# Seven block products for eight in a two-layer graph network's adjacency products, with the order of all engines computed by list scheduling

## The chip, the cores and the metric

The kernel runs on one core of one Trainium2 chip. A core has five engines that matter here, each with a queue of its own that it works through in order: PE (TensorE: matmuls and weight loads), DVE (VectorE), ACT (ScalarE), POOL (GpSimd) and SP, which only issues transfers (DMA). They meet through semaphores. The metric is the device time of one execution in microseconds (us), as a median over runs.

## The reference

There are 64 graphs of 256 nodes with 512 features each. For every graph two layers are computed, both on a normalised and rectified copy of x, and each is added to x:

```python
# layer 0
h = maximum(layernorm(x), 0)
agg = einsum('bij,bjf->bif', adj, h) / maximum(sum(adj), 1e-6)
x = x + relu(concat([h, agg], 2) @ W.T)
# layer 1
h = maximum(layernorm(x), 0)
Xw = h @ Wv + bv
e = leaky_relu((Xw @ aw[:d])[:, None, :] + (Xw @ aw[d:])[:, :, None] + ab, 0.2)
al = adj * exp(e)
transition = al / (sum(al) + 1e-12)
H = 0
for k in range(3):
    H = H + h @ Wk[k] + bk[k]
    h = einsum('bij,bjd->bid', transition, h)
x = x + relu(H)
```

All of it is in fp32. The three products that the change is about multiply a 256 x 256 matrix (the scaled adjacency once, the transition twice) by a 256 x 512 matrix.

## The kernel before, in words

Everything is split by 128 partitions: the 256 nodes into NC = 2 blocks, the 512 features into FC = 4. The nodes are split by parity, so that the last index of a transposed tile such as `h0t` or `ant` says which node block a column belongs to.

A graph goes through these pieces, each a generator whose `yield`s cut it into steps:

- `prepare(g)`: norm of x (`norm_relu`: statistics at L187 on DVE, variance on POOL at L192 and L194, the factor nmr at L197 on DVE, the scaled and rectified copy at L200 on ACT), transposition by 32 x 32 blocks on DVE (L215) and through DRAM (L220 out, L225 back) into `h0t`, and the same for the scaled adjacency (`scaled`, L290 to L296) into `ant`. `blocks` (L233 to L236, POOL) makes four sums of blocks of `h0t`.
- `layer0(g)`: `seven` multiplies h with the two halves of the weight in seven block products of 512 columns (14 matmuls) and leaves one half in `q`, the other in two banks of PSUM; `spread` adds the adjacency times `q` to those banks in four matmuls; L332 adds x and the rectified sum into a new buffer `x1`.
- `turn1(g)`: norm, transposition and block sums of x1, into `h1t`.
- `own(g)`: `seven` with the third-width weights (258 columns: 256 of Wk[0] and one column each for the attention vectors), into `e`; L356 to L359 make `sj` and `si`.
- `transition(g)`: `sj` goes to DRAM and comes back in every partition (`row`); ACT makes two exponentials (L377); DVE takes their maximum (L380), multiplies by the adjacency and sums (L384); ACT scales (L393); the result is transposed through DRAM into `tt`.
- `pair(g)`: `seven` for Wk[2] and Wk[1], into `q1` and two banks.
- `twice(g)`: transition times `q1` onto those banks (`spread`), copies into `u` (L425, ACT), then transition times `u` onto banks that DVE has filled with `e` plus the biases (`seed`, L415), and L433 adds x1 and the rectified sum into `o`, which is stored.

`seven` computes a product of 2 x 2 blocks with seven block multiplications instead of eight. Weights were summed once at the start (`combine`, L93); blocks of h are summed per graph. Partial results stay in three PSUM banks p, r and d, and ACT copies them from one to another between the matmuls (L252, L255, L257, L265). All matmuls of `seven` and `spread` are issued through one helper, so they all carry line 240.

The order on every engine is written out by hand: the strings FIRST, TURN and LAST (L487 to L498) name the pieces by letter and take one step of each in turn; TURN is repeated for the graphs 4 to 63, with up to four graphs in flight. `tc.manual_schedule` keeps that order on all five engines. The setup of the weights stands in `weights_l0` and `weights_l1`; there L159 multiplies two SBUF tiles on DVE, next to POOL's `combine`.

Of the kernel before, what the change touches and what calls it, by code (L numbers as in the profile page):

```python
# [23 lines left out]
def bcast(ap, offset, n):  # L24

    return bass.AP(tensor=ap.tensor, offset=ap.offset + offset, ap=[[0, P], [1, n]])
# [3 lines left out]
def gnn_two_layers(ctx: ExitStack, tc: tile.TileContext, x, adj, w0, wv, bv, aw, ab, wk, bk, out):  # L30

# [7 lines left out]
    const = ctx.enter_context(tc.tile_pool(name="const", bufs=1))  # L56
    loads = ctx.enter_context(tc.tile_pool(name="loads", bufs=3))
    early = ctx.enter_context(tc.tile_pool(name="early", bufs=2))
    small = ctx.enter_context(tc.tile_pool(name="small", bufs=4))
    work = ctx.enter_context(tc.tile_pool(name="work", bufs=1))  # L60
    psum = ctx.enter_context(tc.tile_pool(name="psum", bufs=1, space=bass.MemoryType.PSUM))
    banks0 = [psum.tile([P, F], FP, name=f"bank0_{i}") for i in range(3)]
    banks1 = [psum.tile([P, F], FP, name=f"bank1_{i}") for i in range(3)]
    banks2 = [psum.tile([P, F], FP, name=f"bank2_{i}") for i in range(2)]
    dram = ctx.enter_context(tc.tile_pool(name="dram", bufs=2, space=bass.MemoryType.DRAM))

    X, A = {}, {}

    def load(g, what):
        if what is X:  # L70
            X[g] = loads.tile([P, NC, F], FP, name="x")
            nc.sync.dma_start(X[g], x[g].rearrange("(c p) f -> p c f", p=P))
        else:
            A[g] = loads.tile([P, NC, N], FP, name="a", bufs=4)
            nc.sync.dma_start(A[g], adj[g].rearrange("(c p) j -> p c j", p=P))
# [3 lines left out]
    def forms(name, width):  # L79

        return {k: const.tile([P, FC // 2, width], FP, name=f"{name}_{k}") for k in names}

    B0, B1, B2 = forms("l0", F), forms("l1", F), forms("l1s", HW)
    bk_sb = const.tile([P, F], FP, name="bk_sb")
    c0 = const.tile([P, 1], FP, name="c0")
    ident = const.tile([P, P], FP, name="ident")
    mhalf = const.tile([P, NC], FP, name="mhalf")
    zero = const.tile([P, F], BF, name="zero")

    def combine(b, b12, eng=(nc.vector,) * 4):  # L90

        for e, to, x, y in zip(eng, ("t3", "t1", "t2", "t4"), ("b22", None, "b22", "b21"), (None, "b11", "t1", "t2")):
            e.tensor_sub(b[to], b12 if x is None else b[x], b12 if y is None else b[y])  # L93
            yield

    def turned_on_pe(blocks, banks):

        for i in range(0, len(blocks), FC):
            pt = next(banks).rearrange("p (k n) -> p k n", k=FC)
            for k, block in enumerate(blocks[i : i + FC]):  # L100
                nc.tensor.transpose(pt[:, k, :], block, ident)  # L101
            yield pt

    def weights_l0(w0_sb, b12, banks):

        for side, to in enumerate(((B0["b11"], B0["b21"]), (b12, B0["b22"]))):
            pts = turned_on_pe([w0_sb[oc][:, (side * FC + k) * P :][:, :P] for oc in range(FC) for k in range(FC)], banks)
            for oc, pt in enumerate(pts):
                for kh in range(2):
                    (nc.scalar.copy if oc % 2 else nc.vector.tensor_copy)(to[kh][:, :, oc * P : (oc + 1) * P],  # L110
                                                                         pt[:, 2 * kh : 2 * kh + 2, :])

    def flipped_on_pe(src, width, banks, pool, name, bufs=1):

        t = pool.tile([P, width // P, P, NC], FP, name=name, bufs=bufs)
        for c in range(NC):
            for pt in turned_on_pe([src[:, c, k * P : (k + 1) * P] for k in range(width // P)], banks):
                (nc.scalar.copy if c else nc.vector.tensor_copy)(t[:, :, :, c], pt[:, : width // P, :])
        return t

    def spare(name, bufs=1):

        return work.tile([P, 2, F], FP, name=name, bufs=bufs).rearrange("p s f -> p (s f)")

    def weights_l1():


        aw_sb = spare("x1", 4).rearrange("p (s f) -> p s f", s=2)
        wv_sb = [work.tile([P, NC, 2, HW], FP, name="e", bufs=2).rearrange("p c s w -> p (c s w)")[:, : 2 * F]
                 .rearrange("p (c f) -> p c f", c=2) for _ in range(2)]  # L130
        b12s = spare("u")[:, : FC // 2 * HW].rearrange("p (c w) -> p c w", w=HW)
        b12 = spare("o").rearrange("p (c f) -> p c f", f=F)
        scr, bv_sb = (work.tile([P, F], FP, name=n) for n in ("z0", "z1"))
        two = work.tile([P, FC, P, NC], FP, name="h1t", bufs=2).rearrange("p k n c -> p (k n c)")
        biases = [two[:, :F], two[:, F:], work.tile([P, F], FP, name="tt")]
        vc = small.tile([P, 2, FC], FP, name="vc", bufs=1)
        cc = small.tile([P, 2], FP, name="cc", bufs=1)
        ab_sb = small.tile([P, 1], FP, name="ab_sb", bufs=1)
        src = [wk[k].rearrange("(h c p) o -> h p c o", p=P, h=2) for k in range(NW)]
        nc.sync.dma_start(aw_sb, bcast(aw, 0, 2 * F))  # L140
        for h in range(2):
            nc.sync.dma_start(wv_sb[h], wv.rearrange("(h c p) o -> h p c o", p=P, h=2)[h])
        halves = ((b12s, 0, 1), (B2["b22"], 1, 1), (B2["b11"], 0, 0), (B2["b21"], 1, 0))
        for to, kh, col in halves:
            nc.sync.dma_start(to[:, :, :half], src[0][kh][:, :, col * half : (col + 1) * half])
            nc.gpsimd.memset(to[:, :, half + 1], 0.0)
        yield
        for to, k, kh in ((b12, 2, 0), (B1["b22"], 2, 1), (B1["b11"], 1, 0), (B1["b21"], 1, 1)):
            nc.sync.dma_start(to, src[k][kh])
        nc.sync.dma_start(bv_sb, bcast(bv, 0, F))  # L150
        nc.sync.dma_start(ab_sb, bcast(ab, 0, 1))
        for k in range(NW):
            nc.sync.dma_start(biases[k], bcast(bk, k * F, F))
        yield
        sums = combine(B1, b12, (nc.gpsimd,) * 4)
        for c in range(FC):
            next(sums)
            for s in range(2):
                nc.vector.scalar_tensor_tensor(scr, wv_sb[c // 2][:, c % 2, :], 1.0, aw_sb[:, s, :], op0=ALU.mult,  # L159
                                               op1=ALU.mult, accum_out=vc[:, s, c : c + 1])  # L160
            yield
        for to, kh, col in halves:
            nc.vector.tensor_copy(to[:, :, half], vc[:, col, 2 * kh : 2 * kh + 2])
        yield from combine(B2, b12s)
        for s in range(2):
            nc.vector.scalar_tensor_tensor(scr, bv_sb, 1.0, aw_sb[:, s, :], op0=ALU.mult, op1=ALU.mult,
                                           accum_out=cc[:, s : s + 1])
        nc.vector.scalar_tensor_tensor(c0, cc[:, 0:1], cc[:, 1:2], ab_sb, op0=ALU.add, op1=ALU.add)
        nc.vector.tensor_add(bk_sb, biases[0], biases[1])
        nc.vector.tensor_add(bk_sb, bk_sb, biases[2])  # L170
        yield


    def finished(steps):

        while True:
            try:
                next(steps)
            except StopIteration as end:
                return end.value  # L180

    def norm_relu(src):

        stats = small.tile([P, NC, 6], FP, name="stats")
        mv = small.tile([P, NC, 2], FP, name="mv")
        for c in range(NC):
            nc.vector.bn_stats(stats[:, c, :], src[:, c, :])  # L187
            nc.vector.bn_aggr(mv[:, c, :], stats[:, c, :])  # L188
            if c == 0:
                yield  # L190
        ve = small.tile([P, NC], FP, name="ve")
        nc.gpsimd.tensor_scalar(ve, mv[:, :, 1], LN_EPS, None, op0=ALU.add)  # L192
        rstd = small.tile([P, NC], FP, name="rstd")
        nc.gpsimd.tensor_tensor(rstd, ve, mhalf, op=ALU.pow)  # L194
        yield
        nmr = small.tile([P, NC], FP, name="nmr")
        nc.vector.scalar_tensor_tensor(nmr, mv[:, :, 0], -1.0, rstd, op0=ALU.mult, op1=ALU.mult)  # L197
        h = early.tile([P, NC, F], FP, name="h", bufs=1)
        for c in range(NC):
            nc.scalar.activation(h[:, c, :], src[:, c, :], AF.Relu, bias=nmr[:, c : c + 1],  # L200
                                 scale=rstd[:, c : c + 1])
            yield
        return h

    class Flip:


# [239 lines left out]
    def first(tr_banks):  # L447
# [16 lines left out]
        for _ in range(3):  # L464
            next(sums)
# [82 lines left out]
```

## Time and profile before

| what | value |
|---|---|
| median of 3 runs | 2643.75 us (2642.53 to 2643.8) |
| profiled execution: span | 2643.6 us; the page gives no other time of it |
| PE busy | 2612.3 us, 99% |
| DVE busy | 1204.4 us, 46% |
| ACT busy | 897.2 us, 34% |
| POOL busy | 524.2 us, 20% |
| PE weight loads (PEld) | 1347.6 us, 51%, beside PE's matmuls |
| DMA | 46.3% of 16 engines' time, 112 GB/s to and from memory |
| granted TensorE clock, mean | 0.997 |

Busy time is the union of an engine's instructions in the trace. Matmuls are pipelined: a 512-column fp32 matmul appears as two records, each some 0.59 us long, while the next one starts 0.43 us after it. So the length of a record says little and the distance between starts says much. In a group's row the numbers are: how often, busy us, mean ns of one, and the idle time of the engine just before it with what ended that. For PE the idle time ahead of matmuls is 25 us in all, all but 0.3 of it in the first 150 us.

### The profile page before, as it was taken

To read this page: it belongs to the slowest core of one execution; us is meant where nothing else is said; L and a number is where in the kernel's file an instruction comes from. 1 tells how busy PE (TensorE), PEld (TensorE's weight loads), DVE (VectorE), ACT (ScalarE), POOL (GpSimd) and SP (SyncE) were. 2 spreads that over 40 slices of the span, in tenths; PEclk is the share of its full clock that TensorE was granted. 3 is DMA by queue.
4 is the path that set the end of the run, shared out by engine and by line. 5 is a ranking of instruction groups with operands and counts; after the bars stand their busy time and mean duration, and the time that the engine had idled before them with its cause. 6 is when DMAs were issued, how large, how long until landed. Compare 5 with 4: busy or idle time off the path is not lost.

```text
span 2643.6 us, 23486 instructions
## 1 busy us (share of the span) xinstructions
PE 2612.3 (99%) x6983; PEld 1347.6 (51%) x6983; DVE 1204.4 (46%) x2664; ACT 897.2 (34%) x1807; POOL 524.2 (20%) x785
## 2 busy tenths in 40 slices
PE   7999999999999999999999999999999999999999
PEld 3544555555545545555555455555555554555554
DVE  5544444444444444444444444444444444444433
ACT  2333333333333333333333333333333333333332
POOL 3311211221121112111211221121112112211210
PEclk9999999999999999999999999999999999999999
DMA  5444454454454444444444445444445454454421
GB/s 183 108 126 119 108 118 110 111 123 106 120 120 100 121 115 112 116 111 112 123 103 123 116 103 122 113 112 116 111 114 123 100 125 116 104 122 109 110 74 44
DMA packets 576222, 298.93 MB, mean 113 GB/s; under 512 B 418784, under 2 KB 540640, under 8 KB 576096
## 3 DMA queue, kind: packets, MB, share of 16 engines
q1 hardware_dynamic: 576096, 297.44, 46.3%
q8 instruction: 56, 0.92, 0.1%
q14 instruction: 70, 0.57, 0.1%
HBM read 165.15 MB, written 132.19 MB: 112 GB/s over the span
## 4 chain that ended last, share of the span: by engine, by line
PE 97%; DVE 1%; issue 0%; ACT 0%; DMA 0%; SPq 0%; POOL 0%; DVEq 0%; ACTq 0%
PE bank L240 97%; PE bank L101 0%; DVE z L159 0%; DVE l_t L93 0%; DMA x<-in_x_dram 0%; DMA row<-ds 0%; DVE turned L215 0%; SPq L220 0%; DVE stats L187 0%; ACT z L377 0%; DVE nmr L197 0%; DVE o L433 0%; ACT an L296 0%; DVE l1s_t L93 0%; POOL rstd L194 0%
## 5 line engine op out<-in xcount | busy, mean ns | idle before, releaser
L240 PE MATMUL bank<-l_t,h1t_s 128*128 128x512 f32 x780 | 367.4, 594 | 0.7 <-ACT bank L252 0.7
L240 PE MATMUL bank<-l_t,h0t_s 128*128 128x512 f32 x756 | 356.9, 595 | 4.1 <-DVE l_t L93 3.4
L252 ACT COPY bank<-bank 128x512 f32<-128x512 f32 (+1 forms) x192 | 95.9, 499 | 710.7 <-PE bank L240 710.7
L215 DVE STREAM_TRANSPOSE turned<-h 128x512 f32<-128x512 f32 x252 | 178.4, 709 | 298.0 <-ACT h L200 298.0
L233 POOL TENSOR_TENSOR h0t_s<-h0t 128x256 f32<-128x256 f32 x63 | 53.3, 847 | 982.9 <-DMA h0t<-dh0t 880.3
L240 PE MATMUL bank<-l_b,h1t 128*128 128x512 f32 x520 | 244.4, 592 | 0.1
L240 PE MATMUL bank<-u,tt 128*128 128x512 f32 x512 | 242.1, 596 | 2.3 <-ACT u L425 2.3
L240 PE MATMUL bank<-q,tt 128*128 128x512 f32 x512 | 240.0, 592 | 1.3 <-DMA tt<-dtt 1.3
L240 PE MATMUL bank<-q,ant 128*128 128x512 f32 x512 | 232.5, 596 | 5.3 <-DVE q L275 5.3
L240 PEld LDWEIGHTS bank<-l_t,h0t_s 128*128 128x128 f32 x756 | 143.8, 191 | 183.5 <-issue 169.1
L240 PE MATMUL bank<-l_b,h0t 128*128 128x512 f32 x504 | 237.2, 593 | 0.0
L192 POOL TENSOR_SCALAR ve<-mv 128x2 f32<-128x2 f32 x128 | 29.2, 228 | 1020.4 <-DVE mv L188 1011.8
L200 ACT ACTIVATE h<-x,nmr,rstd 128x512 f32<-128x512 f32 x256 | 202.2, 818 | 17.7 <-DVE nmr L197 17.7
L240 PEld LDWEIGHTS bank<-l_t,h1t_s 128*128 128x128 f32 x780 | 147.7, 190 | 109.7 <-issue 97.0
L240 PEld LDWEIGHTS bank<-l1s_t,h1t_s 128*128 128x128 f32 x768 | 146.5, 191 | 102.7 <-issue 84.1
L240 PE MATMUL bank<-l1s_t,h1t_s 128*128 128x258 f32 x768 | 198.7, 381 | 0.0
L268 DVE TENSOR_TENSOR q<-bank,m 128x512 f32<-128x512 f32 x128 | 88.5, 692 | 202.2 <-PE bank L240 201.2
L332 DVE SCALAR_TENSOR_TENSOR x<-bank,x 128x512 f32<-128x512 f32 x128 | 88.5, 692 | 197.7 <-PE bank L240 197.7
L187 DVE BATCH_NORM_STATS2 stats<-x 128x6 f32<-128x512 f32 x256 | 172.2, 673 | 5.0 <-DMA x<-in_x_dram 5.0
L240 PEld LDWEIGHTS bank<-q,ant 128*128 128x128 f32 x512 | 100.8, 197 | 124.3 <-issue 109.4
L240 PEld LDWEIGHTS bank<-u,tt 128*128 128x128 f32 x512 | 100.6, 197 | 121.5 <-issue 88.4
L240 PEld LDWEIGHTS bank<-q,tt 128*128 128x128 f32 x512 | 100.5, 196 | 120.8 <-issue 116.3
(109 smaller groups left out, 3250.7 us busy)
## 6 DMA issues: line engine op xcount, KB each, us to landing
x<-in_x_dram SPq DMA_DIRECT2D x64, 512.0 KB, 5.6
dh1t<-turned SPq DMA_DIRECT2D x256, 128.0 KB, 2.8
h1t<-dh1t SPq DMA_DIRECT2D x64, 512.0 KB, 3.9
out_dram<-o SPq DMA_DIRECT2D x64, 512.0 KB, 3.2
dh0t<-turned SPq DMA_DIRECT2D x248, 128.0 KB, 2.9
h0t<-dh0t SPq DMA_DIRECT2D x62, 512.0 KB, 4.2
a<-in_adj_dram SPq DMA_DIRECT2D x64, 256.0 KB, 3.2
dant<-turned SPq DMA_DIRECT2D x248, 64.0 KB, 1.9
```

What stands on the lines that cost most here:

```text
L187: nc.vector.bn_stats(stats[:, c, :], src[:, c, :])
L192: nc.gpsimd.tensor_scalar(ve, mv[:, :, 1], LN_EPS, None, op0=ALU.add)
L200: nc.scalar.activation(h[:, c, :], src[:, c, :], AF.Relu, bias=nmr[:, c : c + 1], scale=rstd[:, c : c + 1])
L215: nc.vector.transpose(self.turned.rearrange("p b r c -> p c b r")[:, c], src.rearrange("p c (b s) -> p c b s", s=Q)[:, c])
L233: nc.gpsimd.tensor_add(s1, a21, a22)
L240: nc.tensor.matmul(ps, lhs, rhs, start=start, stop=stop, skip_group_check=True)
L252: nc.scalar.copy(r, p)
L268: nc.vector.tensor_add(c22, p, m167)
L332: nc.vector.scalar_tensor_tensor(x1[:, c, :], banks[1 + c], 0.0, x[:, c, :], op0=ALU.max, op1=ALU.add)
```

## The change

Three things change.

First, the three products per graph with adjacency or transition. `spread` (four matmuls of 512 columns, each two records) goes, and `apply` comes: it treats both factors as 2 x 2 blocks (128 x 128 and 128 x 256) and uses seven matmuls of 256 columns. For that POOL sums blocks of the transposed adjacency or transition (`square`, four operations), DVE takes four differences of blocks of `q`, `q1` or `u` (`tv`), and DVE adds partial results from bank p into the two accumulating banks or into the seed between the matmuls.

```diff
-    def spread(accs, lt, rhs):
-        for k in reversed(range(NC)):
-            for c in range(NC):
-                matmul(accs[c], lt[:, k, :, c], rhs[:, k, :], False, k == 0)
-            yield
+    def apply(tt, q, t, banks, seed):
+        a11, a12, a22, s1, s2, s3, s4 = tt
+        (qt, qk), (tv, tk) = q, t
+        p, r, d = banks
+        st, stk = seed
+        b11, b12, b21, b22 = (qt[:, k, n * half : (n + 1) * half] for k in range(2) for n in range(2))
+        qk0, qk1 = f"{qk}.0", f"{qk}.1"
+        add(*TSUM, lambda: veng.tensor_sub(tv[:, 0], b12, b11), [qk0], [tk + ".0"])                 # L320
+        add(*TSUM, lambda: veng.tensor_sub(tv[:, 2], b22, b12), [qk0, qk1], [tk + ".2"])            # L321
+        add(*TSUM, lambda: veng.tensor_sub(tv[:, 1], b22, tv[:, 0]), [qk1, tk + ".0"], [tk + ".1"]) # L322
+        add(*TSUM, lambda: veng.tensor_sub(tv[:, 3], b21, tv[:, 1]), [qk1, tk + ".1"], [tk + ".3"]) # L323
...
+        mm(p, 0, a11, b11, [qk0], True)
+        mm(p, 1, s1, tv[:, 0], [tk + ".0"])
+        # L331, 256 columns: bank[r] low  = bank[p] low + seed
+        add("DVE", 0.43, lambda: nc.vector.tensor_add(bank[r][:, lo], bank[p][:, lo], st[:, 0, 0]), ...)
+        # L334, 512 columns: seed high (both row blocks) += bank[p] high
+        add("DVE", 0.7, lambda: nc.vector.tensor_add(st[:, :, 1], two(bank[p][:, hi]), st[:, :, 1]), ...)
+        mm(p, 0, s2, tv[:, 1], [tk + ".1"])
+        # L337, 256 columns
+        add("DVE", 0.43, lambda: nc.vector.tensor_add(bank[r][:, hi], bank[p][:, lo], st[:, 0, 1]), ...)
+        mm(r, 0, a12, b21, [qk1])
+        mm(r, 1, s4, b22, [qk1])
+        mm(p, 0, s3, tv[:, 2], [tk + ".2"])
+        # L342, 512 columns
+        add("DVE", 0.7, lambda: nc.vector.tensor_add(bank[d]..., two(bank[p][:, lo]), st[:, 1]), ...)
+        mm(d, 0, a22, tv[:, 3], [tk + ".3"])
+    TSUM = ("DVE", 0.43)
+    veng = nc.vector
```

To serve `apply`, `seven` copies its two other results from the banks to SBUF (`P0`, `P1`) on ACT, and the bias is no longer added on DVE while a bank is seeded (L415 before): POOL adds it to `e` in two operations of 512 columns, behind `si`. In `own`, one copy between banks is replaced by a copy to SBUF and an addition on DVE.

```diff
-        def seed(c):
-            nc.vector.tensor_add(banks1[c]..., e[:, c, :, :half], bk_sb...)
+        for c in range(NC):        # in own, L403
+            add("POOL", 1.3, lambda c=c: nc.gpsimd.tensor_add(et[:, c, :, :half], et[:, c, :, :half], bk_sb...),
+                ["bk", sjk, sik + ".0"], [f"{ek}.{c}0", f"{ek}.{c}1", f"{ek}.{c}"])
```

Second, the order. The strings are gone. Every operation is handed to a `Plan` with its engine, a fixed cost, the names that it reads and writes, a due time for its stage and, for transfers, a lag. `Plan.order` then plays the queues with these costs and takes, whenever an engine is free, the ready operation with the earliest due time; the instructions are issued in that order, fixed for all engines. The plan knows of dependences and costs, not of interference between engines.

```diff
+            for e in free:
+                if ready[e] and free[e] <= now:
+                    _, i = heapq.heappop(ready[e])
+                    cost, lag = self.ops[i][1], self.ops[i][5]
+                    out.append((now, i))
+                    free[e] = now + cost
...
+                        gap = lag or (0.0 if o == e else 0.25 if e == "PE" else 0.08)
...
+    TURN = 40.0
+    def stage(g, offset):
+        plan.due, plan.graph = (g + offset) * TURN, g
+    STAGES = ((loads, 3, -1.71), (prepare, 1, -0.96), (prepared, 1, -0.96), (layer0, 0, -0.61), (turn1, 0, -0.07), (turned1, 0, 1.22), (own_of, -1, 1.31), (transition, -1, 1.53), (moved, -1, 1.30), (pair, -1, 1.44), (twice, -2, 1.65))
```

In a steady turn this gives, on PE, around the second `apply` of `twice` for graph g: the last product of `own(g + 1)` (two matmuls of 258), the last matmul of the first `apply`, two matmuls of the second (`a11`, `s1`), two products of `layer0(g + 3)` (four matmuls of 512), and then the third matmul of the second `apply` (`s2`). DVE has there, in order: the first difference (L320), `sj`, the last addition of `own`, `si` (L400, L401), the other differences (L321, L322, L323), L331, L334. POOL has the two bias additions (L403) and then the block sums of `h1t` (L232).

Third, the buffers. x has six buffers instead of three, and x1 and the result are written over x in the same buffer (`t` in L387 and L444), so the buffers `x1` and `o` go. All tiles come from one pool with fixed numbers of buffers.

## The prediction

> **What bounds the kernel now.** I read the engine shares first, then the chain that ended last, and then asked whether the middle is really full: a table of ten-turn stretches (columns: stretch, its length, busy time and count of PE, PEld, DVE, ACT, POOL, then clock, DMA share, GB/s).
>
> ```profile
> PE 2612.3 (99%) x6983; PEld 1347.6 (51%) x6983; DVE 1204.4 (46%) x2664; ACT 897.2 (34%) x1807; POOL 524.2 (20%) x785
> ...
> PE 97%; DVE 1%; issue 0%; ACT 0%; DMA 0%; SPq 0%; POOL 0%; DVEq 0%; ACTq 0%
> ```
>
> ```profile
> 500.00:904.40 404.40, 404.40 (x1081) 208.78 (x1080) 184.63 (x411) 139.22 (x280) 79.24 (x120) 1.00 0.48 114
> 904.40:1308.80 404.40, 404.40 (x1082) 208.79 (x1080) 184.64 (x411) 139.10 (x280) 79.29 (x120) 1.00 0.46 114
> ```
>
> PE is busy for all of 404.4 us, at full clock, while DVE works 184.6. Busy PE alone would not prove a full PE, so I take the pitch of the matmuls from the timeline (columns: start, us, engine, line, operation):
>
> ```profile
> 1326.89 1.88 PE L240 MATMUL bank<-l_t,h1t 128*128 128x512 f32 x4
> 1328.61 1.03 PE L240 MATMUL bank<-l1s_t,h1t 128*128 128x258 f32 x4
> 1329.48 1.03 PE L240 MATMUL bank<-l1s_b,h1t_s 128*128 128x258 f32 x4
> 1330.35 1.88 PE L240 MATMUL bank<-l_b,h1t_s 128*128 128x512 f32 x4
> ```
>
> One fp32 matmul is two records. Four records of 512 columns take 1.72 us, so a matmul takes 0.858 (1.676 ns a column); four of 258 take 0.87, so 0.437. A graph has 40 of the first and 14 of the second: 34.3 + 6.1 = 40.4 us, which is the turn. 64 turns are 2588; the other 56 us of the span of 2643.6 are filling, first transposes and the end. The page gives no time beside the span; it lies 0.15 under the median of 2643.75, so I add to the span and read the result as a median. A measurement of this kernel can tell about 0.2% (5 us) from no change.
>
> **The skill.** "SBUF — State Buffer", section "Who interferes with whom", says that a VectorE instruction with two SBUF inputs and a GpSimd instruction that reads SBUF exclude each other: the second blocks until the first is through. The trace before agrees, in the setup (DVE, then POOL):
>
> ```profile
> 56.71 0.65 DVE L159 SCALAR_TENSOR_TENSOR z<-e,x 128x512 f32<-128x512 f32 x1
> ...
> 57.40 2.75 DVE L159 SCALAR_TENSOR_TENSOR z<-e,x 128x512 f32<-128x512 f32 x1
> ...
> 60.09 2.28 DVE L197 SCALAR_TENSOR_TENSOR nmr<-mv,rstd 128x2 f32<-128x2 f32 x1
> ```
>
> ```profile
> 57.25 2.35 POOL L93 TENSOR_TENSOR l_t<-l_b,o 128x1024 f32<-128x1024 f32 x1
> 59.56 2.79 POOL L93 TENSOR_TENSOR l_t<-o,l_b 128x1024 f32<-128x1024 f32 x1
> ```
>
> The same L159 takes 0.65 alone and 2.75 where POOL began 0.15 earlier; it ends at 60.15, after POOL's 59.60. The POOL operation that was waiting goes next, and the tiny L197 behind it needs 2.28. So both engines alternate, one operation each, even where one has several ready. In the turns the old kernel hardly meets this.
>
> "TensorE: Matmul & The Clock Gate", section "What's actually happening", says that PE falls to half clock after an idle window of about 3.4 us. The trace shows it even after 2.28 us: four records take 3.57 instead of 1.88.
>
> ```profile
> 134.49 1.04 PE L240 MATMUL bank<-l1s_b,h1t 128*128 128x258 f32 x4
> 137.80 3.57 PE L240 MATMUL bank<-u,tt 128*128 128x512 f32 x4 [2.28 <-ACT u L425]
> ```
>
> **Part 1, the products.** Each product with adjacency or transition was 4 matmuls of 512, 3.43 us; now it is 7 of 256. By the 258 row one takes 0.433, so 3.03. Saved: 0.40 x 3 products x 64 graphs = **77 us**. Bounds: the PEld rows show 190 to 197 ns a load, and a 256-wide record has 217 ns, so loads stay covered; nothing much better or worse than 77. The order of PE confirms seven 256-wide matmuls for each four.
>
> **Part 2, the vector work.** Per graph DVE gains 12 differences of 256 columns (0.42 by L384), 6 additions of 256 (0.43 by the 258 row of L268), 6 of 512 with a repeated bank (0.69 by L268) and one 258-wide addition, and loses two of L415 (0.70): 5.0 + 2.6 + 4.1 + 0.4 - 1.4 = +10.7. From 18.5 it goes to 29.2 of some 40. ACT: four more copies of 0.585, one of 0.38 fewer, 13.9 to 15.9. POOL: sums for two 256 x 256 matrices (0.85 + 0.74 + 0.61 + 0.74 at full width; half to full, I take 1.8 each) and two bias additions of 512 columns (0.74 at 256 and 2.35 at 1024 give 1.28), 7.9 to about 14. No engine passes PE by its sum. The cost is in the waits.
>
> **Part 3, the wait that I expect.** In a steady turn of the new order PE runs: last product of `own`, last matmul of the first `apply` of `twice`, two of the second (0.433 each), two `layer0` products (four matmuls of 0.858), and then a third of the second `apply`, which needs DVE's L334. From the end of `own`'s product PE has 3 x 0.433 + 4 x 0.858 = 4.73 us of work before it. Meanwhile:
> - DVE starts 0.20 after a matmul's slot ends; `e` addition 0.43, `si` (L400) 0.23 + 0.03; POOL, 0.09 later, starts the first bias addition (L403) at 0.98.
> - ACT copies the second half of `u` (0.43 + 0.20 + 0.59); DVE's second difference (L321) is ready at 1.27: after POOL.
> - They alternate. In the traces a blocked operation ends 0.13 to 0.15 sooner than by plain addition. Bias 1 ends at 2.26, L321 at 2.55, bias 2 at 3.68, L322 at 3.97, a block sum (L232, 0.85) at 4.67, L323 at 4.96.
> - L331 and L334 (0.35 and 0.61 of pitch) end at 5.92, and PE starts 0.25 later (0.06 and a weight load): 6.17.
>
> PE waits 6.17 - 4.73 = **1.4 us a turn**. Bounds: 0.9 if L323 gets in before the block sum, 1.0 if L321 wins the first race, 2.0 if operations do not overlap their fixed parts. Over 62 turns: **+87**, 56 to 124. Behind the blocked L321 stand L322, L323, L331, L334 and then the q additions; behind the blocked bias addition stand only block sums for a graph used most of a turn later. Two other meetings, first `apply` of `twice` with the sums of the adjacency, and `layer0` with its block sums, have about 1 us of PE work spare or more; I give them nothing, and up to 0.3 a turn (19 us) as a bound that the range takes in.
>
> **Part 4, the ends.** An `apply` without other PE work is a ping-pong: 0.87 + 0.20 + 1.04 + 0.25 + 0.43 + 0.20 + 0.43 + 0.25 + 1.30 + 0.20 + 0.69 + 0.25 + 0.43 = 6.5 for 3.4 before. Four at the end lie nearly bare, two more half: 5 x 3.1 = 16, and some waits there are long enough for half clock, +6: **+22** (10 to 35). At the start two bare ones add 6, while the old start idles 25 us in gaps that an order by readiness may fill: 0, plus or minus 10.
>
> **Part 5, at nothing.** One buffer for x, x1 and the result: `out` reads what the next load overwrites, but with six buffers nearly two turns (80 us) lie between, against 3.2 + 5.6 us of transfers. The DMAs per graph are the same in number and bytes; SP's order moves them with half of the DMA time free. If that cover failed, `x` would be late first, at L178, by a few us once a graph.
>
> **Sum:** 2643.6 - 77 + 87 + 22 = **2676**; with the wait's bounds 2645 to 2713.
>
> **Rivals.**
> - A, the lock is harmless: DVE's differences go back to back or find POOL idle. For it: L415 and POOL meet each turn now with PE never idle. Against: POOL's two long additions start just before L321 in the order, every turn. Then 2643.6 - 77 + 22 = 2589, to 2610 with small waits: faster. It decides at a wait of (77 - 22) / 62 = 0.9 us a turn.
> - B, DVE falls behind: waits at all three meetings and DVE near 90%. At 2.4 us a turn 2643.6 - 77 + 149 + 22 = 2738; if such waits also halve the clock each turn (1.7 us lost), 2843. For it: 29.2 us of DVE in order with blocked operations between. Against: some 10 us a turn in which DVE has nothing to do.
> - C, the seven-product form saves nothing since 256-wide matmuls cost more than their columns: against it stands the 258 row. It would give 2643.6 + 87 + 22 = 2753; I hold it at 2%.
>
> **Numbers.** Likeliest case 0.52, A 0.28, B 0.18, C 0.02. The low end is A's, 2590; the high end goes into B, 2765, leaving out some 2 in 10. Likeliest case alone: 2645 to 2713. Faster by over 0.2%: A and the lowest edge of the likeliest, 0.30; within: 0.06; slower: 0.64.
>
> **What would show it.** Right: PE idle about 1.4 us a turn, nearly all at one matmul of the second `apply`, released by L334; L321 to L323 and L403 each 0.3 to 1 us longer than alone; 256-wide records 217 ns apart; a turn of 40.6. Wrong: turns of 39.3 with PE full (A); the idle time spread over many matmuls, or half clock in the turns (B).

## The result, and the profile after

| | before | after |
|---|---|---|
| median | 2643.65 us (2642.53 to 2643.8) | 2704.35 us (2701.96 to 2708.55) |
| span of the profiled execution | 2643.6 us | 2701.2 us |
| PE busy | 2612.3 us, 99% | 2563.3 us, 95% |
| first transfer of a result / last | 144.7 / 2639.9 us | 132.4 / 2697.5 us |

After to before is 1.023 (95% interval 1.0215 to 1.0244): slower. The page after, its engine shares and the chain that ended last:

```profile
PE 2563.3 (95%) x8133; PEld 1554.8 (58%) x8133; DVE 2024.6 (75%) x4136; ACT 1036.9 (38%) x1999; POOL 949.8 (35%) x1425
...
PE 73%; DVE 19%; DMA 5%; issue 2%; SPq 1%; POOL 1%; ACT 0%; DVEq 0%; ACTq 0%; POOLq 0%
```

PE has less to do than before (the products did get cheaper), yet DVE stands in 19% of the chain where it stood in 1%. The table of stretches says that this is so in the middle too (columns as before: stretch, length, PE, PEld, DVE, ACT, POOL, clock, DMA share, GB/s):

```profile
400.00:1200.00 800.00, 773.28 (x2472) 473.02 (x2472) 614.26 (x1249) 315.50 (x607) 287.85 (x430) 1.00 0.45 112
```

PE stands still for 26.7 of 800 us at full clock, where before it stood still for none. For what, the waits of PE say (engine and line, who released it, us in total, times, the longest):

```profile
PE bank L250 <- DVE e L334: 81.3, 61, 3.6
PE bank L250 <- DVE bank L342: 18.1, 28, 2.2
PE bank L250 <- POOL s L232: 10.7, 1, 10.7
```

One wait, once in nearly every graph, at the third matmul of the second `apply` of `twice`. Here it is in one turn, on PE, then on DVE, then on POOL (start, us, engine, line, operation):

```profile
656.07 0.59 PE L250 MATMUL bank<-t,st 128*128 128x256 f32 x2
656.51 1.88 PE L250 MATMUL bank<-l_b,h0t 128*128 128x512 f32 x4
658.22 1.88 PE L250 MATMUL bank<-l_t,s 128*128 128x512 f32 x4
661.43 0.70 PE L250 MATMUL bank<-t,st 128*128 128x256 f32 x2 [1.33 <-DVE e L334]
```

```profile
655.87 1.25 DVE L400 TENSOR_SCALAR si<-e,c 128x2 f32<-128x2 f32 x1
657.16 1.10 DVE L401 TENSOR_SCALAR si<-si 128x2 f32<-128x2 f32 x1
658.17 0.41 DVE L321 TENSOR_TENSOR t<-u 128x256 f32<-128x256 f32 x1
658.51 1.06 DVE L322 TENSOR_TENSOR t<-u,t 128x256 f32<-128x256 f32 x1
659.60 0.84 DVE L323 TENSOR_TENSOR t<-u,t 128x256 f32<-128x256 f32 x1
660.36 0.42 DVE L331 TENSOR_TENSOR bank<-bank,e 128x256 f32<-128x256 f32 x1
660.70 0.68 DVE L334 TENSOR_TENSOR e<-bank,e 128x512 f32<-128x512 f32 x1
```

```profile
655.92 2.31 POOL L403 TENSOR_TENSOR e<-e,bk_sb 128x512 f32<-128x512 f32 x2 [5.84 <-DVE e L266]
658.19 1.10 POOL L232 TENSOR_TENSOR s<-h1t 128x256 f32<-128x256 f32 x1
659.37 0.79 POOL L232 TENSOR_TENSOR s<-s,h1t 128x256 f32<-128x256 f32 x1
```

A matmul's slot is the time from its start to that of the next one where PE is full. PE's two `layer0` products fill 3.44 us (two pitches of 1.72) and end their slots at 658.22 + 1.72 = 659.94; the next matmul starts at 661.43, so 1.49 us are lost, 1.33 of it shown as a wait. On DVE the two tiny operations on 128x2 elements (L400, L401) take 1.25 and 1.10 us beside POOL's two bias additions, and two of the differences take 1.06 and 0.84 beside block sums; L321, the same kind of subtraction, takes 0.41, and there it is POOL's block sum, begun 0.02 us after it, that takes 1.10 where the next ones take 0.79. An operation that takes two to six times what its shape costs, with a POOL operation over the same time, is the thing to look for in such a listing.

Turns, taken from one store of a result to the next, are mostly 40.80 us in the first half; before they were 40.44. In 23 turns of 41.3 to 41.8 a second wait is added, at an L342. In 18 of them, all in the second half, it is the L342 of the first `apply` of `twice` (DVE, then PE):

```profile
1759.92 1.30 DVE L194 STREAM_TRANSPOSE turned<-h 128x512 f32<-128x512 f32 x2 [1.21 <-DMA dh<-turned]
1761.15 0.67 DVE L342 TENSOR_TENSOR bank<-bank,p 128x512 f32<-128x512 f32 x1
```

```profile
1760.18 1.03 PE L250 MATMUL bank<-l1s_b,s 128*128 128x258 f32 x4
1761.87 0.71 PE L250 MATMUL bank<-t,tt 128*128 128x256 f32 x2 [0.66 <-DVE bank L342]
```

DVE waits 1.21 us for the transfer out of the only `turned` buffer before it may transpose the next block into it, and L342, for which PE waits, stands behind that transposition. In the other five, among the first turns, it is the L342 of `layer0`'s product, and DVE stood 1.5 to 2.2 us in L352, waiting for the load of the adjacency.

### The profile page after: what moved, and what is told of

Read it like the earlier page. It is cut to its first block, busy times and chain, and to the rows that moved or that the text cites. A ratio compares the mean times of both kernels' runs of the same rounds, so it can differ in the third digit from the quotient of the medians.

```text
span 2701.2 us, 28155 instructions
## 1 busy us (share of the span) xinstructions
PE 2563.3 (95%) x8133; PEld 1554.8 (58%) x8133; DVE 2024.6 (75%) x4136; ACT 1036.9 (38%) x1999; POOL 949.8 (35%) x1425
## 3 DMA queue, kind: packets, MB, share of 16 engines
q8 instruction: 65, 1.06, 0.2%
## 4 chain that ended last, share of the span: by engine, by line
PE 73%; DVE 19%; DMA 5%; issue 2%; SPq 1%; POOL 1%; ACT 0%; DVEq 0%; ACTq 0%; POOLq 0%
PE bank L250 73%; DVE si L400 3%; DMA dh<-turned 3%; DVE t L322 3%; DVE si L401 2%; DVE t L323 2%; DVE turned L194 1%; DVE e L334 1%; DVE t L321 1%; DVE e L266 1%; DMA a<-in_adj_dram 1%; DVE bank L331 1%; SPq L198 1%; DVE bank L342 1%; DVE q L266 1%
## 5 line engine op out<-in xcount | busy, mean ns | idle before, releaser
L250 PE MATMUL bank<-l_t,s 128*128 128x512 f32 x1536 | 722.7, 594 | 13.1 <-POOL s L232 10.7
L250 PEld LDWEIGHTS bank<-l_t,s 128*128 128x128 f32 x1536 | 291.3, 190 | 251.0 <-issue 217.9
L250 PE MATMUL bank<-t,st 128*128 128x256 f32 x768 | 237.0, 390 | 82.6 <-DVE e L334 81.3
L232 POOL TENSOR_TENSOR s<-h0t 128x256 f32<-128x256 f32 x126 | 106.9, 848 | 563.0 <-DMA h0t<-dh 405.0
L263 ACT COPY p<-bank 128x512 f32<-128x512 f32 x256 | 149.8, 585 | 350.2 <-PE bank L250 348.9
L403 POOL TENSOR_TENSOR e<-e,bk_sb 128x512 f32<-128x512 f32 x128 | 148.3, 1180 | 370.5 <-DVE e L266 370.4
L250 PEld LDWEIGHTS bank<-t,st 128*128 128x128 f32 x768 | 141.6, 191 | 176.4 <-DVE e L334 131.1
L250 PE MATMUL bank<-l_b,s 128*128 128x512 f32 x512 | 240.6, 592 | 0.0
L263 ACT COPY m<-bank 128x512 f32<-128x512 f32 x256 | 149.8, 585 | 223.5 <-PE bank L250 223.5
L250 PE MATMUL bank<-l1s_t,s 128*128 128x258 f32 x768 | 198.7, 381 | 0.0
L194 DVE STREAM_TRANSPOSE turned<-h 128x512 f32<-128x512 f32 x252 | 164.5, 689 | 25.8 <-DMA dh<-turned 21.6
L250 PEld LDWEIGHTS bank<-l1s_t,s 128*128 128x128 f32 x768 | 146.2, 190 | 46.9 <-issue 24.6
L444 DVE SCALAR_TENSOR_TENSOR x<-bank,x 128x512 f32<-128x512 f32 x128 | 88.5, 691 | 87.4 <-PE bank L250 81.5
```

Source lines behind the costliest of these rows:

```text
L194: add("DVE", 0.71, lambda c=c: nc.vector.transpose(u.rearrange("p b r c -> p c b r")[:, c], s.rearrange("p c (b s) -> p c b s", s=Q)[:, c] ...
L232: lambda i=i, f=f, p=p, q=q: getattr(nc.gpsimd, f)(s[:, i], p, q),
L250: nc.tensor.matmul(ps, lhs, rhs, start=start, stop=stop, skip_group_check=True)
L263: add("ACT", 0.21 + 0.00073 * width, lambda: nc.scalar.copy(dst, bank[b][:, :width]), [f"bank{b}"], dkeys)
L403: add("POOL", 1.3, lambda c=c: nc.gpsimd.tensor_add(et[:, c, :, :half], et[:, c, :, :half], bk_sb.rearrange("p (s f) -> p s f", s=2)), ["b ...
L444: add("DVE", 0.69, lambda c=c: nc.vector.scalar_tensor_tensor(t[:, c, :], bank[banks[1 + c]], 0.0, t[:, c, :], op0=ALU.max, op1=ALU.add), ...
```

## The experiments

Times are medians, and ratios are to the kernel before on the same chip. Line numbers shift by a few lines where an edit adds lines; the text says which line is meant.

### e1: the bias additions no longer meet `si` and the differences

```diff
-  add("POOL", 1.3, lambda c=c: nc.gpsimd.tensor_add(et[:, c, :, :half], et[:, c, :, :half], bk_sb...),
+  add("POOL", 1.3, lambda c=c: (nc.gpsimd.memset(bk_sb, 0.0), nc.gpsimd.memset(bk_sb, 0.0)),
```

> Each of the two bias additions on POOL (L403) is replaced by two memsets of the bias tile, so POOL is occupied at the same places but reads nothing; the bias is left out of the result. The order of all engines stays. Lock theory (a DVE operation that needs the shared read port and a POOL operation that reads take turns): the two small operations L400 and L401, 1.25 and 1.10 us in the changed kernel, fall to 0.23 and 0.17, only the block sums still meet L322 and L323, PE's wait for L334 falls from 1.3 us a turn to 0 to 0.3, and the time to about 2620 us; if the two small operations are held up by writing operations too, about 2655. Queue theory (DVE is late because too much work stands in its queue, whatever POOL does): the wait stays at 1.3 us and the time at 2700.

Measured: 2650.97 us, 1.0029 (1.0012 to 1.0047), so 53 us less than the change. The wait at L334 is nearly gone (its row in PE's waits), and DVE's groups (count, busy us, mean ns) show why:

```profile
PE bank L250 <- DVE e L334: 5.2, 3, 2.0
```

```profile
L400 DVE TENSOR_SCALAR si<-e,c 128x2 f32<-128x2 f32 x64 | 15.0, 234 | 2.3
L401 DVE TENSOR_SCALAR si<-si 128x2 f32<-128x2 f32 x64 | 11.9, 185 | 2.2
```

In the change they are

```profile
L400 DVE TENSOR_SCALAR si<-e,c 128x2 f32<-128x2 f32 x64 | 79.3, 1239 | 2.3
L401 DVE TENSOR_SCALAR si<-si 128x2 f32<-128x2 f32 x64 | 69.4, 1084 | 2.2
```

The order on PE, DVE and ACT is operation by operation that of the change, so it isn't that DVE has too much in its queue; what it meets on POOL decides. The wait fell by 76 us and the time by 53, which misses the 2620: other waits grew (`q` from 2.2 to 12.1 us, `p` at L334 from 2.0 to 6.8), and the differences of the other two products got longer (the mean of their L322 rose from 514 to 707 ns). One limit of this experiment: a memset doesn't need `e`, so POOL runs it some 5 us earlier in the turn. It shows what the meeting costs, not that reading is what blocks. The kernel leaves the bias out of its result.

### e2: the differences of the second `apply` take one operand from PSUM

```diff
-        add(*TSUM, lambda: veng.tensor_sub(tv[:, 1], b22, tv[:, 0]), [qk1, tk + ".0"], [tk + ".1"])
-        add(*TSUM, lambda: veng.tensor_sub(tv[:, 3], b21, tv[:, 1]), [qk1, tk + ".1"], [tk + ".3"])
+        add(*TSUM, lambda: veng.tensor_sub(tv[:, 1], y22, tv[:, 0]), ...)   # y: u's values, still in the banks
+        add(*TSUM, lambda: veng.tensor_sub(tv[:, 3], y21, tv[:, 1]), ...)   # L320, L321 likewise
```

> In the second apply of twice the four differences (L320 to L323) take one operand from the PSUM bank in which u still stands, instead of from u in SBUF; results are the same. Lock theory: L322 and L323 fall from 1.06 and 0.84 to 0.43 us, L400 and L401 stay at 1.25 and 1.10, PE's wait for L334 falls by about 1.0 us a turn, the time to about 2640. Queue theory: the same number of operations of the same length stands in DVE's queue, so nothing moves: 2700.

Measured: 2661.41 us, 1.006 (1.0041 to 1.0079); the profiled execution is the fastest of the four, 2651. The order is that of the change on every engine, only the operands of the differences differ. The last two of them take 408 and 424 ns (999 and 798 in the change), and PE's wait for L334 (here L336) falls by 60 us:

```profile
PE bank L250 <- DVE e L336: 20.8, 61, 3.6
```

```profile
L324 DVE TENSOR_TENSOR t<-bank,t 128x256 f32<-128x256 f32 x64 | 26.1, 408 | 0.0
L325 DVE TENSOR_TENSOR t<-bank,t 128x256 f32<-128x256 f32 x64 | 27.2, 424 | 2.2
```

`si` still takes 1206 and 1084 ns. So with the differences free 60 of the 81 us go; the 0.34 us a turn that stay come from the blocked `si` ahead of them. A difference with one SBUF input isn't blocked. The shares don't add up: e10 below frees `si` and 75 us go, since the differences then also start before most of the block sums (L322's mean is 547 ns there).

### e4: a condition in the plan that should hold POOL back

```diff
+                ["bk", sjk, sik + ".0"] + gate(g - 1), ...     # bias additions "after" L323
+        sums1[g] = blocks(of(H1T, g), of(S1, g), gate(g - 2))
```

> The bias additions (L403) and the block sums of h1t on POOL wait until the last difference (L323) of the second apply of twice is done; nothing else moves on PE. Lock theory: all of L400, L401, L321, L322, L323 fall to their lengths alone, PE's wait for L334 goes to 0 and the time to about 2615, with what is left of waits for L342. Queue theory: no change on DVE, 2700; if the later block sums hold up PE instead, slower than 2704.

Measured: 2705.47 us, 1.0234, as the change. The edit failed as an edit: POOL's queue came out in the same order but for the last graphs, and its first bias addition still starts when `e` is complete, since a condition in the plan makes no semaphore. It says nothing of the lock. It does say why the prediction's timing of that addition was off: the change itself names `si` among what the bias additions wait for in the plan, and on the chip they don't wait for it: L403 starts at 655.92, while L400 has run since 655.87.

### e6: two buffers for the transposed blocks

```diff
-    X = buf("x", [NC, F], 6)
+    X = buf("x", [NC, F], 5)
-    TURNED = buf("turned", [F // Q, Q, NC], 1)
+    TURNED = buf("turned", [F // Q, Q, NC], 2)
...
-        put(norm_relu(g, of(X, g), next(norms)), F, TURNED[0], of(D["h1"], g))
+        put(norm_relu(g, of(X, g), next(norms)), F, TURNED[1], of(D["h1"], g))
```

> The transposition buffer of 512 features, one for both layers in the changed kernel, becomes two, one for each layer (x has five buffers for six to make room). Second wait theory (DVE stands in L194 until the transfers out of that buffer are through, 21.6 us in all, and L342 of the first apply behind it is late for PE, 18.1 us in 28 turns): both waits go, the turns are all 40.8, the time falls by 18 to 25 us to about 2682. Rival (L342 is late for the same lock as L334): no change within 5 us.

Measured: 2680.32 us, 1.0139 (1.0122 to 1.0156). The size was as expected, by luck, since the reason was not. DVE's wait for the transfer is gone, but the plan gave another order of all engines, and the waits changed places:

```profile
PE bank L250 <- DVE bank L342: 65.0, 55, 3.4
...
PE bank L250 <- DVE e L334: 6.8, 3, 3.6
```

In 50 of the 55 cases the L342 is that of the second `apply` and stands behind L419 and L444 in DVE's queue. So this run doesn't test whether the one buffer was what made L342 late in the change; that stays a reading of the trace.

### e10: the bias additions behind the block sums of `h1t`

```diff
+        behind = [key] if key in plan.writer else []      # key: the last block sum of h1t
+            add("POOL", 1.3, ...the same addition..., ["bk"] + behind, ...)
-    ORDER = (1, 3, 2, 4, 5, 10, 6, 9, 7, 0, 8)
+    ORDER = (1, 3, 2, 4, 5, 6, 10, 9, 7, 0, 8)
```

> The two bias additions stand behind the block sums of h1t in POOL's own queue (its order, not a semaphore), so they begin only when that transfer has landed; the result is complete. Lock theory: L400 and L401 fall to 0.23 and 0.17 us as in the run with memsets, L321 to L323 still meet the block sums, PE's wait for L334 falls from 81 us to below 20 and the time to about 2650. Queue theory: as before, 2704.

Measured: 2642.7 us, 1.0001 (0.9988 to 1.0015). Here the order in POOL's queue was changed, and that does hold: `si` falls to 266 and 213 ns, PE's wait for L334 (here L335) to 5.8 us:

```profile
PE bank L251 <- DVE e L335: 5.8, 3, 2.0
```

```profile
L401 DVE TENSOR_SCALAR si<-e,c 128x2 f32<-128x2 f32 x64 | 17.0, 266 | 2.3
L402 DVE TENSOR_SCALAR si<-si 128x2 f32<-128x2 f32 x64 | 13.6, 213 | 2.2
```

POOL still does both bias additions on the same data, and PE, DVE, ACT and the transfers do the same operations in the same order as in the change. Only where the additions stand in POOL's queue has changed, and that returns all of the loss of 60 us.

### e12: no meeting at all in the second `apply`

This is e10, e2 and a later due time for `combine` of the second layer's weights, which moves the first block sum ahead of L454:

```diff
+        plan.due = 20.0      # before combine("l1"), -30.0 again behind it
```

> Bias additions behind the block sums, the differences of the second apply from PSUM, and the first sums of the weights of layer 1 on POOL (L454) with a later due time, so that the first graph's block sums are not behind them. Lock theory: PE's wait for L334 is gone (under 5 us), the wait of 10.7 us for the first block sum falls to about 3, the rest are waits for L342 behind L194; about 2630, faster than the kernel before. Queue theory: 2690 to 2700.

Measured: 2641.14 us, 0.9996 (0.9984 to 1.0009), not to be told from e10, and not the 2630 expected. The wait for the first block sum went from 10.4 to 4.2 us, but PE then waits 5.8 us for L179 (`mv`), and the first result comes 4.9 us later than in e10. Many turns are 39.20 us exactly, 40.44 - 39.20 = 1.24 less than before, which is what 3 x 0.41 us on the products give (8 records 0.429 us apart for 14 that are 0.216 apart). The mean of the first 58 turns is 39.90, as PE still waits for L342 (17.1 us in all), for `q` and others. And at the end the clock is at half for 33 us.

### e11: e12 with two buffers for the transposed blocks

The edit is that of e6.

> As the run before it, and two transposition buffers (five x buffers). Lock theory and the second wait theory together: turns of 39.3 to 39.6 us, about 2600. If two transposition buffers only move the wait to another place, as the run with them alone did (L342 65 us there), 2630 or more.

Measured: 2672.84 us, 1.011 (1.0093 to 1.0127): 32 slower than e12. PE's wait for L342 went up to 55.6 us in 59 turns. As in e6 the buffer gave DVE nothing to wait for, and the order that the plan made from it was worse. Which entry of that order is at fault was not tried.

### e5: the list order and the buffers with eight products

```diff
-        mm(p, 0, a11, b11, [qk0], True)
...
-        mm(d, 0, a22, tv[:, 3], [tk + ".3"])
+        for c in range(NC):
+            add("ACT", 0.585, lambda c=c: nc.scalar.copy(bank[banks[1 + c]]..., st[:, c]), ...)
+        for k in range(NC):
+            for c in range(NC):
+                add("PE", 0.86, lambda k=k, c=c: matmul(bank[banks[1 + c]], tt[k][c][0], qt[:, k], False), ...)
```

> The changed kernel with its list scheduling and buffers, but each product with adjacency or transition again as four matmuls of 512 columns; ACT copies the seed to the banks, the differences, block sums of the 256 x 256 matrices and DVE additions of apply are gone; results are the same. If the order by list scheduling costs nothing by itself: turns of 40.4 as before, 2640 to 2660, so that all of the loss is the price of the seven products. If the computed order is worse in itself: above 2680. Lock theory adds that L400 and L401 are still long here, with no one on PE waiting for them.

Measured: 2646.41 us, 1.0011 (1.0003 to 1.002). The stretch shows PE full again, and the turns are 40.44:

```profile
400.00:1200.00 800.00, 800.00 (x2139) 413.21 (x2138) 399.16 (x794) 382.66 (x733) 198.33 (x279) 1.00 0.44 114
```

In this kernel `si` still takes 1247 and 1102 ns, and DVE waits 100 us for transfers out of `turned` (21.6 in the change). Neither makes PE wait: in the eight-product form no DVE operation stands between the matmuls of a product. So the list order and the buffers by themselves cost next to nothing, 0.1%; the loss belongs to the seven products, whose matmuls depend on DVE's differences and additions in between.

### e17: the change, with a plan that knows the port

```diff
+                while ready[e] and self.ops[ready[e][0][1]][6] and port > now + 1e-9:
+                    held.append(heapq.heappop(ready[e]))     # op[6]: any on POOL; on DVE two SBUF inputs, or small
...
+                if self.ops[i][6]:
+                    port = free[e]
...
-                        gap = lag or (0.0 if o == e else 0.25 if e == "PE" else 0.08)
+                        gap = lag or (0.0 if o == e else 0.2 if e == "PE" else 0.25 if o == "PE" else 0.08)
...
-                parts(uk), [f"{dk}.{q}"], 2.6 if width == F else 2.0)
+                parts(uk), [f"{dk}.{q}"], 3.2 if width == F else 2.0)
```

The operations are those of the change. What the plan assumes is new: POOL and such DVE operations exclude each other; a result reaches PE 0.25 us after its end (0.08 before), and one of PE's reaches the others after 0.20 (0.25 before); a transfer out of `turned` takes 3.2 us (2.6 before); a bias addition takes 1.2 (1.3 before).

> The changed kernel as it was (bias additions behind si, differences from SBUF, the end as it was), with nothing but the plan's knowledge changed: POOL operations and DVE operations with two SBUF inputs, or small tensor_scalar ones, may not overlap, an engine behind PE starts 0.20 us after it, a transfer out of the transposition buffer takes 3.2 us. If the loss was only that the plan did not know of the port: PE's wait for L334 below 20 us, about 2635. If the meeting must go by itself, since POOL on the chip starts the bias additions before si, which the plan takes for a condition and the chip does not: the wait stays above 40 us, about 2680.

Measured: 2623.28 us, 0.9922 (0.9905 to 0.9938): 81 us faster than the change, and faster than before. The wait at L334 is gone, and the largest that is left is that for the first block sum (11.4 us). In a turn DVE now does the differences and L346, L349 (L331 and L334 of the change) first and `si` behind them:

```profile
1047.10 0.42 DVE L337 TENSOR_TENSOR t<-u,t 128x256 f32<-128x256 f32 x1
1047.56 0.42 DVE L338 TENSOR_TENSOR t<-u,t 128x256 f32<-128x256 f32 x1
1047.90 0.42 DVE L346 TENSOR_TENSOR bank<-bank,e 128x256 f32<-128x256 f32 x1
1048.24 0.68 DVE L349 TENSOR_TENSOR e<-bank,e 128x512 f32<-128x512 f32 x1
1048.84 0.41 DVE L279 TENSOR_TENSOR e<-bank,ms 128x258 f32<-128x258 f32 x1
1049.29 1.25 DVE L415 TENSOR_SCALAR si<-e,c 128x2 f32<-128x2 f32 x1
1050.57 1.10 DVE L416 TENSOR_SCALAR si<-si 128x2 f32<-128x2 f32 x1
```

`si` is blocked as much as ever, 1.25 and 1.10 us, where PE doesn't wait for it. The differences find the port free: 0.42 each. PE's order is new too: the last product of `own`, on which `si` depends, now stands behind the second matmul of this `apply`, so that other products cover 4.30 us there and not 3.43. Which of the assumptions does how much, and how much is the better cover, was not separated.

### e14: e12 with that plan, and e15: the last two graphs with eight products

The edit of e14 is that of e17, on e12. That of e15, on e14 (the first product of `twice` likewise):

```diff
+        whole = g >= G - 2
+        if whole:
+            apply8(of(TT, g), U[0], banks, (et[:, :, :, :half], ek))     # four 512-column matmuls
+        else:
             apply(at, U[0], of(T, next(ts)), banks, (et[:, :, :, :half], ek), True)
```

> As the run without meetings (e12), and the plan itself is told what the runs showed: POOL operations and DVE operations with two SBUF inputs, or small tensor_scalar ones, may not overlap; an engine behind PE starts 0.20 us after it, not 0.08; a transfer out of the transposition buffer takes 3.2 us, not 2.6. Lock theory: the order then has the remaining meetings (L321 to L323 of the other two products, 0.65 to 0.7 us for 0.42) and the late L342 off PE's path; turns of 39.2 to 39.4, about 2610. If what is left is the scatter of the transfers, which no plan knows: about 2640 as e12.

> As e14, and twice of the last two graphs uses four matmuls of 512 columns, as nothing is left there to cover the back and forth between PE and DVE. End theory: the last four turns fall from some 143 us in e12 to 132 as with eight products; 10 us less than e14. If the end is set by the transition of the last graph: no gain.

Measured: e14 2621.73 us, 0.9909 (0.9892 to 0.9925); e15 2596.63 us, 0.9818 (0.9804 to 0.9833), the fastest of all. e14 is 12 over the 2610 expected. That e14 and e17 can't be told apart says that once the plan has these data, where the bias stands and where the differences read from hardly matter. The step to e15 is 25.1 us where 10 were expected. The last 80 us of each, as stretches, e14 and then e15:

```profile
2540.00:2620.00 80.00, 59.21 (x146) 30.57 (x145) 30.89 (x66) 15.71 (x32) 6.57 (x10) 0.78 0.07 22
```

```profile
2516.00:2596.00 80.00, 71.97 (x214) 39.37 (x212) 32.97 (x77) 29.63 (x59) 10.12 (x14) 1.00 0.20 50
```

At the end of e14 the clock is 0.78 and PE is busy 59 of 80 us; at that of e15 it is 1.00 and 72. The last two turns take 22.99 and 20.03 us for 35.23 and 35.17.

### e16: e12 with that end

The edit is that of e15.

> e12 with the same change of the last two graphs alone: by the end theory 10 us under e12, about 2631; otherwise 2641.

Measured: 2659.86 us, 1.0055 (1.0039 to 1.0071), 19 slower than e12 (16 by the ratios; the two ran on different chips). The end did get shorter as in e15 (last two turns 23.83 and 23.72 for 34.43 and 36.22), but the mean of the first 58 turns rose from 39.90 to 40.64, although PE, DVE, ACT and POOL do the same in the same order there. PE waits more often for `q` (17.9 us in 34 turns, 4.0 in 9 in e12). Why a steady turn takes another course with the same order I can't say, and it stays open; e12's single executions also lie between 2634.8 and 2652.3.

## Why the prediction was right, and where it was not

The forecast was 2676 us, the measurement 2704; the direction, the place and the mechanism were right, and the sum was 28 short.

- **Part 1, the products (77 us): right.** Turns of 40.44 with eight products (e5) and of 39.20 with seven where PE is full (e12) give 1.24 us a graph, 79 us. The 256-wide records are 216 ns apart in the mean, for 217 predicted. Rival C is out.
- **Part 2, no engine passes PE by its sum: right.** In the stretch of 800 us DVE was busy for 614 (31 us a turn, blocked time included), ACT for 316 and POOL for 288.
- **Part 3, the wait: right in place, releaser and size, wrong in its detail.** Predicted were 1.4 us a turn; the trace has 1.49 by slots in the turn above, 1.45 in the mean, 1.33 as shown. The step that failed is that the first bias addition starts behind L400. POOL starts when `e` is complete, beside L400, and e4 showed why: the order is fixed, but `si` is nothing that POOL waits for. So the two bias additions blocked L400 and L401, of which I had the first at 0.23 us and free and the second not in the sum, and not L321, which ran at 0.41. Nor was L403 lengthened: it took 1.18 us, and I had it at 1.28 alone. Then the block sums blocked L322 and L323. I had expected L321, L322 and L323 to be blocked, and it was L400, L401, L322 and L323; that L334 ended at nearly the predicted time is luck in the detail, not in the mechanism. Freeing the differences (e2) takes 60 of the 81 us away, freeing `si` (e10) 75, so the two aren't shares of one sum. The Trainium skill, "SBUF — State Buffer", section "Who interferes with whom", also names `tensor_scalar` among the operations that can take the shared pair, under conditions that it sends the reader elsewhere for; I had read the line on two inputs and not that one. The traces agree: 1239 and 1084 ns beside POOL's additions, 234 and 185 without.
- **"Two other meetings", given nothing: the term that was missing.** PE's waits at L342 are 18.1 us as shown. Of these, 12.1 are in the 23 turns named above, 15.8 by slots. That is within the 19 us which the prediction allowed these two products, but by luck: what makes L342 late there isn't a meeting over the port. In 18 cases DVE stands in L194 for the one `turned` buffer, in five in L352 for a load. The other 6 us are at the start and the end; only in the longest, 2.24 us in the last turns, does L342 stand behind a blocked `si` (1.25 and 1.10 us). All this is read from the trace; e6 changed the order and so didn't test it. Part 5 had put the transfers at nothing, from the free share of the DMA time; it didn't ask which engine waits for a buffer with something urgent behind it.
- **Part 4, the ends: 22 predicted, 17 found.** The last five turns take 178.0 us after and 161.0 before. e15 shows what those ping-pongs can cost with another order: 25 us. The start comes out even (the first result is 12.3 us sooner, but before, the turn that followed it took 29.34 us, 11.1 less than the others), though PE waits 10.7 us there for the first block sum (L232) behind `combine`.
- **The sum.** A turn became 41.16 - 40.44 = 0.72 us longer in the mean of 58, predicted was (87 - 77) / 62 = 0.16: 32 us between. Against full turns of 39.20 those 58 lose 113 us: 90 at L334 (1.45 a turn at the wait, and 0.10 because the second record of that matmul then starts 0.32 us after the first and not 0.22), 18 at L342 reckoned the same way, and 5 elsewhere. At 1.40 a turn L334 would have been 81, so the 32 us are 9 from L334, 18 from L342 and 5 small ones. With 5 less at the ends and 1 less at the start 26 are explained; the profiled execution is 25 over the forecast (2701 for 2676), and the median another 3.
- **Rival A** (the lock is harmless) is refuted by e1 and e10, and its number was near what can be had: 2589 to 2610 where e15 has 2597, by taking the meetings off the path. That nearness is no test of its sum, as e15 also has another end. **Rival B** (DVE behind at all three meetings) is out: DVE is at 75%, and the clock in the turns is 1.00.
- **A reading of the trace before.** The L159 that the prediction calls alone (0.65 us) ran beside a POOL operation too, L194 on 128x2 elements (56.58 to 57.29), and wasn't held up by it. What follows from that is below.

## What to carry to other kernels

Before a saving on the full engine is counted, list every operation of another engine that it makes this engine wait for, and look at what else holds those operations: a port shared with POOL, and a buffer that an operation ahead in the same queue is waiting for, count as much as the operation's own time. A scheduler that gets exclusions and latencies as data gave 81 us with the same operations; the plan that only listed dependences put the colliding operations side by side every turn, and a condition in it that no semaphore carries holds nothing back. Where the pipeline runs dry, the form with fewer waits can be the better one even if it has more matmul work (e15: 25 us).

## What the runs showed of the hardware that I had not expected

**A tiny operation pays in full for a blocked port.** 128x2 elements take 0.23 and 0.17 us alone and 1.25 and 1.10 beside POOL's additions of 1.18 us: the wait has the length of the other engine's operation, whatever the size of its own. The other way round it isn't so: in e17 six subtractions of 128x256 with both inputs in SBUF began inside a POOL operation on 128x2 elements (L194), with up to 0.65 us of it to go, and took 0.41 to 0.43 us. Nor do the recorded starts tell who goes first: L400 began 0.04 us ahead of L403 and was held, L321 began 0.02 ahead of a block sum and held it.

**Half clock without a long wait.** "TensorE: Matmul & The Clock Gate", section "What's actually happening", in the Trainium skill has the clock fall after an idle window of about 3.4 us. In the last turns of the changed kernel a wait of 3.56 us is followed by half clock, but so is one of 2.24; a wait of 2.00 is not, and half clock also follows a series of waits of 1.28 and 0.53 us with single matmuls between. The second and the third case, on PE:

```profile
2654.85 0.59 PE L250 MATMUL bank<-t,st 128*128 128x256 f32 x2
2657.68 1.22 PE L250 MATMUL bank<-t,tt 128*128 128x256 f32 x2 [2.24 <-DVE bank L342]
2658.70 1.06 PE L250 MATMUL bank<-u,tt 128*128 128x256 f32 x2
...
2692.21 0.70 PE L250 MATMUL bank<-t,st 128*128 128x256 f32 x2 [2.00 <-DVE e L334]
```

Two records of the same shape take 1.06 us behind the wait of 2.24, 0.59 ahead of it. The three stretches at half clock before the last matmul are 6.8, 3.4 and 3.4 us long; what decides whether a wait brings one was not found. e14 spent 35 us of its end like this, and e15 none before its last matmul.
